# Writes of zeros on GpSimd between indirect DMAs, counted by the planner

## The chip, the cores and the metric

The kernel runs on one core of a Trainium2 chip. Five engines work side by side, each on its own queue in order: TensorE (PE) for matrix products, VectorE (DVE) and ScalarE (ACT) for elementwise work and reductions, GpSimd (POOL), and SyncE (SP), which here issues most of the DMAs. An engine waits for another through semaphores. DMAs move data between the chip's main memory and the core's SBUF, and land some time after they are issued. An *indirect* DMA takes a list of row numbers and reads or writes one row of a table per partition; in this kernel POOL issues all of those.

The metric is the time of the kernel on the device in microseconds (us), as the median of several runs. A profile is one execution that is recorded instruction by instruction; it has a time of its own.

## The reference

The input is 8 blocks of 512 tokens, each token a vector of 128 numbers. Three steps follow each other, each with a residual:

```python
x = x + 0.5 * ffn(layernorm(x))
x = x + attn(layernorm(x))
x = x + 0.5 * ffn(layernorm(x))
```

with

```python
def ffn(x):                       # 8 experts, one for each token
    xn  = rms_norm(x) * scale
    ids = argmin(distance(xn, centroids))
    for e in range(8):
        a, g = split(xn @ up_w[e])            # 128 -> 2 x 256
        y = (a * silu(g)) @ down_w[e]         # 256 -> 128
        out = where(ids == e, y, out)
    return out + x

def attn(x):                      # a decaying sum along the 512 tokens of a block
    r, k, v = split(x @ W_rkv + b_rkv)
    r, k = sigmoid(r), exp(k)
    u1, u2 = scan(lam, k * v), scan(lam, k)   # y[t] = lam * y[t-1] + u[t]
    return ((u1 + gamma * k * v) / (u2 + gamma * k + 1e-6) * r) @ W_o + b_o
```

All is in float32. A token uses one expert only, so the kernel sorts tokens by expert and computes each once.

## The kernel before, in words

**Tables.** The first ffn works on two tables of tokens (table 0 holds blocks 0 to 3, table 1 blocks 4 to 7), the second on one (table 2, all eight blocks, routed in the batches 0 and 1, 2 and 3, 4 and 5, 6, 7). For each batch the kernel normalises (moments on DVE, roots on ACT and a Newton step on POOL, L508 to L511, or DVE), compares with the centroids on PE, and ranks the tokens of each expert, which gives every token a row in a table in main memory. `scatter` (L720) writes the rows there: one indirect DMA on POOL for 128 tokens, four for each block. The tokens of an expert then lie in whole tiles of 128 rows; eight zero fills on SP (L830), at addresses that come with the last routing of a table, pad the last tile of each expert.

**Experts.** A table's tiles are worked on in pairs (`pair`). SP loads the tokens (`xg`, L892) and the expert's weights (`wup`, L899); PE transposes (L905), multiplies by the first weights (L910); ACT and DVE form `a * silu(g)` (L942, L947); PE multiplies by the second weights (L918). Pairs 0 to 11 belong to table 0, 12 to 23 to table 1, 24 to 43 to table 2, which is taken in four parts of 8, 8, 4 and 19 tiles as its batches are routed. For tables 0 and 1 the results go to a table of results through SP (L984), and `finish` gathers them back in token order: four indirect DMAs on POOL for each block (L997), then one addition on DVE (L1006). For table 2 `send` (L961) writes each tile straight to the output with one indirect DMA on POOL.

**Attention** runs between, for blocks 0 and 1, 2 and 3, 4 and 5, 6, 7: projections on PE, exponentials on ACT, two scans and eight further passes on DVE.

**The order.** No engine's order is written by hand. Each piece of work is handed to a planner (`Plan.add`) with the engines that could do it, a cost in us on each, what it reads and writes, and a lag for a DMA's landing. `Plan.schedule` simulates the five queues with these costs: it takes the piece that can start first, with a priority between those that can start nearly at once. `Plan.trace` does this for 48 settings of three parameters (how long to wait for the preferred engine, for a change of ACT's table, and how near two starts count as equal), keeps the order with the shortest simulated span, and issues the instructions in it. So a change of costs on one engine can move work on all. A scatter, a gather and a send cost 1.3 each there.

Of the kernel before, what the change touches and what calls it, by code (L numbers as in the profile page):

```python
# [10 lines left out]
F32 = mybir.dt.float32  # L11
# [8 lines left out]
class Buf:  # L20


    def __init__(self, make, tag=None):
        self.make, self.tag, self.tile = make, tag, None
        self.writers, self.readers = [], []
# [5 lines left out]


class Op:
    def __init__(self, ways, reads, writes, order, lag, table):
        self.ways, self.order, self.lag, self.table = ways, order, lag, table
        self.bufs = list(dict.fromkeys(list(reads) + list(writes)))
        self.needs, self.users = set(), []


class Plan:  # L40
# [8 lines left out]

    HOP, SWITCH = 0.1, 1.28

    def __init__(self, slots, load_table):
        self.ops, self.slots, self.load_table = [], slots, load_table

    def add(self, ways, reads=(), writes=(), order=None, part=False, lag=0.0, table=None):
        op = Op(ways, reads, writes, order or {}, lag, table)
        for b in reads:
            op.needs.update(b.writers)  # L60
            b.readers.append(op)
        for b in writes:
            op.needs.update(b.readers)
            if not (part and not b.readers):
                op.needs.update(b.writers)
            if b.readers or not part:
                b.readers, b.writers = [], []
            b.writers.append(op)
        op.needs.discard(op)
        self.ops.append(op)  # L70

    def schedule(self, spare, wait, slack):

        left, ready, uses = {}, {}, {}
        for op in self.ops:
            left[op], ready[op] = len(op.needs), 0.0
            for b in op.bufs:
                uses[b] = uses.get(b, 0) + 1
        slots = {tag: [0.0] * n for tag, n in self.slots.items()}
        free, held, released, table = {}, set(), {}, None  # L80
        waiting = [op for op in self.ops if not op.needs]
        order, span = [], 0.0
        while waiting:
            could = []
            for op in waiting:
                at = ready[op]
                for b in op.bufs:
                    if b.tag and b not in held:
                        if not slots[b.tag]:
                            break  # L90
                        at = max(at, min(slots[b.tag]))
                else:
                    for n, (engine, cost, call) in enumerate(op.ways):
                        then = max(at, free.get(engine, 0.0))
                        if n == 0 or free.get(op.ways[0][0], 0.0) > then + spare:
                            if op.table not in (None, table):
                                then += wait
                            could.append((then, engine, cost, call, op))
            if not could:
                return None  # L100
            first = min(could, key=lambda c: c[0])
            start, engine, cost, call, op = min(
                (c for c in could if c[1] == first[1] and c[0] <= first[0] + slack),
                key=lambda c: (c[4].order.get(c[1], c[4].index), c[0]),
            )
            load = None
            if op.table not in (None, table):
                load = table = op.table
                cost += max(0.0, self.SWITCH - wait)
            order.append((op, call, load))  # L110
            for b in op.bufs:
                if b.tag and b not in held:
                    slots[b.tag].remove(min(slots[b.tag]))
                    held.add(b)
            waiting.remove(op)
            free[engine] = start + cost
            end = start + cost + op.lag
            span = max(span, end)
            for b in op.bufs:
                uses[b] -= 1  # L120
                released[b] = max(released.get(b, 0.0), end)
                if uses[b] == 0 and b.tag:
                    slots[b.tag].append(released[b] + self.HOP)
            for u in op.users:
                left[u] -= 1
                ready[u] = max(ready[u], end + self.HOP)
                if left[u] == 0:
                    waiting.append(u)
        return span, order

    def trace(self):
        for i, op in enumerate(self.ops):
            op.index = i
            for n in op.needs:
                n.users.append(op)
        orders = [
            self.schedule(spare, wait, slack)
            for spare in (0.0, 0.5, 1.0, 3.0) for wait in (0.0, 0.4, 0.8, 1.28)
            for slack in (0.05, 0.1, 0.2)
        ]  # L140
        span, order = min((o for o in orders if o), key=lambda o: o[0])
        for _, call, load in order:
            if load:
                self.load_table(load)  # L144
            call()
        return span

# [2 lines left out]
def kernel(  # L150
# [37 lines left out]
    nc = tc.nc  # L188
    B, L, D = x_in.shape
    E, _, H2 = up_w.shape  # L190
    H = H2 // 2
    P = 128
# [14 lines left out]
    ROW = 2 * D + 4  # L207
# [8 lines left out]
    const = ctx.enter_context(tc.tile_pool(name="const", bufs=1))  # L216
# [79 lines left out]
    slots = {}  # L296
# [19 lines left out]

    small_d = part_of(ps_small, "d", 0, TMAX * E, 128 // (TMAX * E))
    small_r = part_of(ps_small, "r", 128, E * (TMAX + 1), RBUF)
    plan = Plan(slots, nc.scalar.preload_act_table_set)
    add = plan.add  # L320
    FIRST, LATE = -10**6, 10**6
    EXP, SILU = "natural_log_exp_and_others", "silu_and_others"
# [40 lines left out]
    rows = const.tile([E + 1, P], F32, tag="rows", name="rows")  # L363
# [177 lines left out]
    class Table:  # L541
# [33 lines left out]
        order = 0  # L575
# [74 lines left out]
    def route(table, batch, near, rows):  # L650
# [8 lines left out]
        posi = buf(route_p, [P, TMAX], I32, "posi", n, 3)  # L659
# [66 lines left out]
        for i, b in enumerate(batch):  # L726
            there = Buf(None)
            table.parts.append(there)
            row = Buf(lambda b=b: xrow[b]) if table.f else rows[i][0]
            for t in range(NT):  # L730
                add([("POOL", 1.3, lambda row=row, t=t, q=i * NT + t: scatter(row, t, q))],
                    [posi] + rows[i], [there], part=True, lag=2.4)

    def take(table, m: int):

# [137 lines left out]
    def pair(k, table, parts, keep, spots, at_, downs, downs_, tiles, start):  # L873
        n = len(tiles)
        f, row, early = table.f, table.row, table.left > 0
        xg = buf(work, [P, 2, ROW], F32, "xg", k, 7)
# [7 lines left out]
        y = buf(work, [P, 2, D], F32, "ys", k, 4)  # L884
# [38 lines left out]
        for i, j in enumerate(tiles):  # L923
            add([("SP", 0.52, lambda i=i, j=j: rows(i, j))], [at_] + parts, [xg], {"SP": LATE + k},
                part=True, lag=2.3)
        for i, j in enumerate(tiles):
            add([("SP", 0.52, lambda i=i, j=j: weights(i, j))], [at_], [wup], {"SP": LATE + k},
                part=True, lag=3.8)
# [25 lines left out]
        if f:  # L954
            add([("DVE", 0.1 + 0.18 * n, lambda: nc.vector.scalar_tensor_tensor(  # L955
                y()[:, :n, :], half(), 0.5, xg()[:, :n, D : 2 * D], ALU.mult, ALU.add))],
                [ps_y, xg], [y], soon)

            def send(i):
                nc.gpsimd.nop()  # L960
                inst = nc.gpsimd.indirect_dma_start(  # L961
                    out=out.rearrange("b l d -> (b l) d"),
                    out_offset=bass.IndirectOffsetOnAxis(
                        ap=xg()[:, i, 2 * D : 2 * D + 1].bitcast(I32), axis=0),
                    in_=y()[:, i, :], in_offset=None, bounds_check=TOKENS - 1, oob_is_err=False,
                ).ins
                tc.declare_no_dep(inst, group="out", reason="each token is in one row")
                tc.add_to_no_dep_group("out", inst)

            for i in range(n):  # L970
                add([("POOL", 1.3, lambda i=i: send(i))], [y, xg], [], lag=2.5)
            return
        add(
            [
# [17 lines left out]
    def finish(table, b: int):  # L992

        yg = buf(work, [P, NT, D], F32, "yg", b, 4)

        def gather(t):
            nc.gpsimd.indirect_dma_start(  # L997
                out=yg()[:, t, :], out_offset=None, in_=table.result()[:, :],
                in_offset=bass.IndirectOffsetOnAxis(
                    ap=table.posi[:, table.blocks.index(b), t : t + 1], axis=0),  # L1000
            )

        for t in range(NT):
            add([("POOL", 1.3, lambda t=t: gather(t))], [table.result, table.posi_], [yg], part=True,
                lag=2.0)
        add([("DVE", 0.68, lambda: nc.vector.tensor_add(xb[b], yg(), xb[b]))], [half_[b], yg], [x_[b]])  # L1006

    def attention(batch):
# [108 lines left out]
    for i, (f, batches, taken) in enumerate(TABLES):  # L1117
        Table.order = i * LATE // 8
        table = Table(f"t{i}", f, [b for batch in batches for b in batch])
# [44 lines left out]
```

## Time and profile before

| | us |
|---|---|
| median of 3 timed runs | 330.13 |
| lowest, highest | 328.52, 331.52 |
| profiled execution, its own time | 374.23 |
| its span, first to last instruction | 372.5 |
| PE busy in the span | 245.3 |
| DVE busy | 179.9 |
| ACT busy | 165.0 |
| POOL busy | 162.8 |
| of it, 135 indirect DMAs (32 + 32 + 32 + 39) | 139.7 |

The mean granted clock of PE was 0.864 of full speed in the profiled execution. Busy times are of the engine itself; SP has none, since it only issues. A line of the timeline gives start and duration in us, engine, line of the code, operation, what is written from what, shapes, and in brackets the idle time of the engine before it and what ended it. "issue" means that nothing in the profile explains the idle time; "remote" means a semaphore whose setter the profile does not show. The view of waits sums idle times by who waited and who ended it. The view by stretches gives busy times of the engines in windows of the span.

### The profile page before, as it was taken

How to read it: one execution, taken by the hardware profiler on the slowest of the kernel's cores; microseconds unless marked ns; L12 is line 12 of the kernel's file. 1: busy time of each engine (PE TensorE's matmuls, PEld its weight loads, DVE VectorE, ACT ScalarE, POOL GpSimd, SP SyncE). 2: the span in 40 equal slices, each digit the busy share in tenths (PEclk: the TensorE clock that was granted, in tenths of full speed). 3: DMA queues.
4: the chain of work that ended last, by engine and by line, in shares of the span. 5: the costliest groups of instructions: out<-in, count | busy, mean ns of one | idle time of the engine just before them, and what ended most of it. 6: DMA issues, size and time to landing. Idle time of an engine off the chain costs nothing. (4 is left out here: it accounts for less than half of the span.)

```text
span 372.5 us, 5675 instructions
## 1 busy us (share of the span) xinstructions
PE 245.3 (66%) x1510; PEld 201.6 (54%) x1510; DVE 179.9 (48%) x607; ACT 165.0 (44%) x355; POOL 162.8 (44%) x244
## 2 busy tenths in 40 slices
PE   4754635089966921998772985569971457997871
PEld 3644525089866911965351632229761356996761
DVE  4583882022211121467996979766875502232230
ACT  4881880234332301589723867634882311232230
POOL 5277457300000474110187578810277652465545
PEclk9999998569999975899987788768996577899997
DMA  8611372167767843620011125351045547787710
GB/s 225 172 43 42 89 231 76 60 195 226 209 192 234 261 138 104 189 72 28 22 37 42 35 73 171 127 143 58 0 136 186 150 168 231 242 257 230 226 56 17
DMA packets 46226, 50.25 MB, mean 135 GB/s; under 512 B 6095, under 2 KB 32739, under 8 KB 46194
## 3 DMA queue, kind: packets, MB, share of 16 engines
q1 hardware_dynamic: 41334, 39.31, 35.5%
q0 software_dynamic: 4832, 10.56, 8.4%
q8 instruction: 13, 0.21, 0.3%
q14 instruction: 19, 0.16, 0.2%
q10 hardware_dynamic: 28, 0.01, 0.0%
HBM read 36.00 MB, written 14.31 MB: 135 GB/s over the span
## 5 line engine op out<-in xcount | busy, mean ns | idle before, releaser
L910 PE MATMUL h<-xgT,wup 128*128 128x128 f32 x680 | 94.5, 295 | 11.4 <-DMA wup<-in_L_ffn_up_w_dram 7.1
L910 PEld LDWEIGHTS h<-xgT,wup 128*128 128x128 f32 x680 | 89.5, 211 | 13.9 <-issue 10.4
L947 DVE TENSOR_TENSOR sg<-h,sg 128x512 f32<-128x512 f32 (+1 forms) x44 | 29.2, 671 | 117.0 <-ACT sg L942 107.1
L997 POOL DMA_INDIRECT yg<-yt,pt x32 | 36.3, 1133 | 83.1 <-DMA xg<-t 55.7
L918 PE MATMUL ps_xy<-wsb,sg 128*128 x340 | 50.4, 294 | 32.8 <-ACT xgT L933 20.0
L918 PEld LDWEIGHTS ps_xy<-wsb,sg 128*128 128x128 f32 x340 | 44.7, 204 | 37.7 <-ACT xgT L933 25.7
L961 POOL DMA_INDIRECT out_dram<-ys,xg x39 | 38.5, 986 | 43.0 <-DVE ys L955 25.2
L942 ACT ACTIVATE sg<-h 128x512 f32<-128x512 f32 (+1 forms) x44 | 25.2, 582 | 66.8 <-PE h L910 37.9
L933 ACT ACTIVATE xgT<-ps_xy,cols 128x256 f32<-128x256 f32 (+1 forms) x44 | 20.5, 465 | 48.6 <-remote 17.3
L720 POOL DMA_INDIRECT t<-xn,posi_t x32 | 31.1, 971 | 16.2 <-issue 8.1
L720 POOL DMA_INDIRECT t<-xrow,posi_t x32 | 33.8, 1055 | 9.9 <-issue 8.2
L905 PE MATMUL ps_xy<-ident,xg 128*128 128x128 f32 x85 | 19.9, 312 | 25.0 <-ACT xgT L933 13.4
L619 PE MATMUL ps_small<-cw,xT 128*128 128x8 f32 x128 | 22.9, 309 | 10.1 <-issue 4.6
L619 PEld LDWEIGHTS ps_small<-cw,xT 128*128 128x128 f32 x128 | 21.9, 260 | 14.2 <-issue 7.5
L905 PEld LDWEIGHTS ps_xy<-ident,xg 128*128 128x128 f32 x85 | 11.9, 157 | 29.1 <-ACT xgT L933 14.1
L1105 PEld LDWEIGHTS side_o<-wo_sb,num 128*128 128x128 f32 x64 | 10.8, 243 | 16.1 <-DVE num L1070 11.6
L445 ACT ACTIVATE xrow<-x,nra,rs 128x128 f32<-128x128 f32 x32 | 13.1, 482 | 14.4 <-issue 6.7
L473 DVE BATCH_NORM_STATS2 bn_f<-x 128x6 f32<-128x128 f32 x64 | 13.5, 277 | 10.6 <-ACT x L462 6.6
L975 ACT ACTIVATE ys<-ps_xy 128x256 f32<-128x256 f32 (+1 forms) x24 | 9.0, 375 | 21.6 <-PE ps_xy L905 9.3
L1105 PE MATMUL side_o<-wo_sb,num 128*128 128x128 f32 x64 | 11.0, 328 | 10.0 <-DVE num L1070 10.0
L508 POOL TENSOR_TENSOR tr<-va,yr 128x8 f32<-128x8 f32 (+1 forms) x11 | 2.7, 241 | 30.2 <-ACT yr L500 26.1
L144 ACT ACT_TABLE_LOAD x12 | 15.4, 1283 | 0.2
(166 smaller groups left out, 382.2 us busy)
## 6 DMA issues: line engine op xcount, KB each, us to landing
wup<-in_L_ffn_up_w_dram SPq DMA_DIRECT2D x85, 256.0 KB
xg<-t SPq DMA_DIRECT2D x39, 130.0 KB
xg<-t SPq DMA_DIRECT2D x46, 64.0 KB
yt<-ys SPq DMA_DIRECT2D x22, 128.0 KB
x<-in_L_attn_inputs_dram SPq DMA_DIRECT2D x8, 256.0 KB
t<-fill SPq DMA_DIRECT2D x9, 130.0 KB
t<-fill SPq DMA_DIRECT2D x18, 64.0 KB
wsb<-in_L_ffn_down_w_dram SPq DMA_DIRECT2D x8, 128.0 KB
```

The source lines that it names most:

```text
L144: self.load_table(load)
L619: nc.tensor.matmul(ps_d()[:, ts(i * NT + t, E)], xT()[:, ts(t, P)], cw, start=True, stop=True)
L720: ordered(table, nc.gpsimd.indirect_dma_start(out=table.at()[:, :], out_offset=bass.IndirectOffsetOnAxis(ap=posi()[:, q : q + 1], axis=0), ...
L905: nc.tensor.transpose(ps_x()[:, ts(i, P)], xg()[:, i, :D], ident)
L910: nc.tensor.matmul(hp()[:, i, ts(c, P)], wup()[:, i, ts(c, P)], xgT()[:, ts(i, P)], start=True, stop=True,)
L918: nc.tensor.matmul(ps_y()[:, ts(i, D)], sg()[:, i, ts(c, P)], wdown[c][:, ds(expert(downs[j]) * W, D)], start=(c == 0), stop=(c == NHC - 1),)
L933: ("ACT", 0.2 + 0.13 * n, lambda: nc.scalar.activation(xgT()[:, : n * P], ps_x()[:, : n * P], AF.Copy, scale=scale_c)),
L942: [("ACT", 0.16 + 0.22 * n, lambda: nc.scalar.activation(sg()[:, :n, :], hp()[:, :n, H:], AF.Silu))],
L947: [("DVE", 0.1 + 0.28 * n, lambda: nc.vector.tensor_mul(sg()[:, :n, :], hp()[:, :n, :H], sg()[:, :n, :]))],
L961: inst = nc.gpsimd.indirect_dma_start(out=out.rearrange("b l d -> (b l) d"), out_offset=bass.IndirectOffsetOnAxis(ap=xg()[:, i, 2 * D : 2 ...
L997: nc.gpsimd.indirect_dma_start(out=yg()[:, t, :], out_offset=None, in_=table.result()[:, :], in_offset=bass.IndirectOffsetOnAxis(ap=table. ...
L1105: nc.tensor.matmul(ps_o()[:, ts(t, P)], num()[:, ts(i * NT + t, P)], wo_sb, start=False, stop=(t == NT - 1),)
```

## The change

The planner learns of rows of indirect DMAs. An operation has a new mark, `row`, which scatters, gathers and sends carry. While planning, a marked operation that starts less than 0.65 us after POOL came free counts as one more of a row, otherwise as the first of a new one. In front of the fifth of a row the plan puts a pause of 1.3 us on POOL and counts anew. Unmarked work on POOL in between does not by itself end a row. When the instructions are issued, a pause is a `memset` of 128 partitions by 1536 float32 zeros on POOL into a tile that nothing reads. Since the pause delays the start of the operation in the simulation, it takes part in the choice among the 48 orders, and the order on all engines is another one. In the code of the change, numbers of lines are 9 to 11 higher.

```diff
-    HOP, SWITCH = 0.1, 1.28
-
-    def __init__(self, slots, load_table):
-        self.ops, self.slots, self.load_table = [], slots, load_table
-
-    def add(self, ways, reads=(), writes=(), order=None, part=False, lag=0.0, table=None):
-        op = Op(ways, reads, writes, order or {}, lag, table)
+    HOP, SWITCH, ROW, PAUSE = 0.1, 1.28, 4, 1.3
+
+    def __init__(self, slots, load_table, pause):
+        self.ops, self.slots, self.load_table, self.pause = [], slots, load_table, pause
+
+    def add(self, ways, reads=(), writes=(), order=None, part=False, lag=0.0, table=None, row=False):
+        op = Op(ways, reads, writes, order or {}, lag, table, row)
...
-            order.append((op, call, load))
+            pause = False
+            if op.row:
+                row = row + 1 if start < free.get(engine, 0.0) + self.PAUSE / 2 else 1
+                if row > self.ROW:
+                    pause, row = True, 1
+                    start += self.PAUSE
+            order.append((call, load, pause))
...
-        for _, call, load in order:
+        for call, load, pause in order:
             if load:
                 self.load_table(load)
+            if pause:
+                self.pause()
             call()
...
-    plan = Plan(slots, nc.scalar.preload_act_table_set)
+
+    idle = const.tile([P, 3 * L], F32, tag="idle", name="idle")
+    plan = Plan(slots, nc.scalar.preload_act_table_set, lambda: nc.gpsimd.memset(idle, 0.0))
...
-                    [posi] + rows[i], [there], part=True, lag=2.4)
+                    [posi] + rows[i], [there], part=True, lag=2.4, row=True)
...
-                add([("POOL", 1.3, lambda i=i: send(i))], [y, xg], [], lag=2.5)
+                add([("POOL", 1.3, lambda i=i: send(i))], [y, xg], [], lag=2.5, row=True)
...
-                lag=2.0)
+                lag=2.0, row=True)
```

More of the change, by code (lines that the diff above doesn't have):

```diff
@@ L33, with __init__ @@
 class Op:
-    def __init__(self, ways, reads, writes, order, lag, table):
-        self.ways, self.order, self.lag, self.table = ways, order, lag, table
+    def __init__(self, ways, reads, writes, order, lag, table, row):
+        self.ways, self.order, self.lag, self.table, self.row = ways, order, lag, table, row
         self.bufs = list(dict.fromkeys(list(reads) + list(writes)))
@@ L81, in schedule @@
         waiting = [op for op in self.ops if not op.needs]
-        order, span = [], 0.0
+        order, span, row = [], 0.0, 0
         while waiting:
```

## The prediction

> **What bounds the kernel now.** I read the timed runs against the profiled execution, then the waits, then the stages one by one in the timeline. The first comparison sets the tone: the profiled execution took 374.23 us (span 372.5), the timed runs 328.52 to 331.52, median 330.13. The profiled one is 44.1 us longer, so before a wait in it is costed, it must be asked whether the timed runs have that wait at all. The view of waits, filtered to waits whose releaser the profile can't name ("remote"), with columns total, times and longest:
>
> ```profile
> ACT xgT L933 <- remote: 17.3, 1, 17.3
> ...
> ACT sg L942 <- remote: 14.2, 2, 10.1
> ...
> DVE slot_t L703 <- remote: 8.4, 2, 4.9
> ...
> ACT ys L975 <- remote: 7.9, 1, 7.9
> ...
> ACT xT L462 <- remote: 6.7, 1, 6.7
> ```
>
> They sum to 54.5 us; DVE's 4.9 and ACT's 6.7 are the same stretch (30 to 38 us), so 49.6. The timeline of ACT shows the longest, and that of POOL what runs beside it:
>
> ```profile
> 54.68 0.47 ACT L933 ACTIVATE xgT<-ps_xy,cols 128x256 f32<-128x256 f32 x1 [0.78 <-PE ps_xy L905]
> 72.47 0.47 ACT L933 ACTIVATE xgT<-ps_xy,cols 128x256 f32<-128x256 f32 x1 [17.31 <-remote]
> ```
>
> ```profile
> 44.17 1.01 POOL L720 DMA_INDIRECT t<-xn,posi_t  x1 [0.15 <-issue]
> 45.48 0.99 POOL L720 DMA_INDIRECT t<-xn,posi_t  x1 [0.30 <-issue]
> 49.65 0.96 POOL L720 DMA_INDIRECT t<-xn,posi_t  x1 [3.18 <-DVE near L642]
> 50.91 0.95 POOL L720 DMA_INDIRECT t<-xn,posi_t  x1 [0.30 <-issue]
> ```
>
> From 49.65 POOL issues 16 indirect DMAs in a row, 1.26 us apart, until 69.6. After the fourth or fifth, everything else stands: PE's transposes for the third pair are issued at 57.85, ACT answers at 72.47, when the row has ended and landed. In the same stretch register moves on SP take 0.7 us each where they take 0.03 elsewhere. The other "remote" waits also lie in or just behind POOL's rows (128 to 147 beside 16 gathers, 335 to 339 beside five sends). POOL itself keeps its 1.26 us. This is what the added writes can interrupt, and the whole forecast hangs on whether it exists without the profiler. 49.6 us of such waits and an excess of 44.1 us nearly cancel: the simplest account is that the stalls are the profiled execution's own, and that at most 5.5 us of these waits are in a timed run, if nothing else was dearer under the profile.
>
> With them taken out, the timed run is: routing to about 50; experts of the first two tables, bound by PE and the weight loads; attention, DVE 80 to 93% busy; then 16 pairs of experts as a tail.
>
> ```profile
> 80.00:90.00 10.00, 10.00 (x90) 10.00 (x90) 2.08 (x3) 4.49 (x10) 0.00 (x0) 0.99 0.72 222
> ...
> 180.00:190.00 10.00, 6.65 (x23) 2.65 (x22) 9.26 (x9) 4.94 (x8) 4.52 (x4) 0.97 0.14 40
> ...
> 350.00:360.00 10.00, 8.33 (x75) 8.14 (x74) 2.96 (x6) 2.40 (x5) 5.47 (x6) 1.00 0.43 130
> ```
>
> The columns after the length are PE, PE's weight loads, DVE, ACT and POOL. POOL bounds none of these stages through its total; it bounds the hand-overs: first expert, first attention, last send.
>
> **The change, part by part.** The price of one pause. The trace has no memset of 128x1536, but two smaller ones on POOL: 128x128 takes 0.20 us and 128x256 takes 0.30, so 0.10 per 128 columns, and 0.20 + 11 x 0.10 = 1.30 us. Their start-to-start distances (0.15 and 0.26) give 0.15 + 11 x 0.11 = 1.36. It also takes the place of the 0.30 us that POOL spends between two indirect DMAs: where four small operations stand between two of them now, 0.03 + 0.16 us are idle instead. Net 1.30 + 0.19 - 0.30 = 1.2 us. The new order holds 30 of them: 7 among the 32 scatters of the first two tables, 6 among the gathers, 9 among the last table's scatters and the sends between them, 8 in the sends behind the last scatter. That is 39 us of POOL work (its busy time from 163 to about 202), of which only what a hand-over waits for counts.
>
> *First experts.* The scatters of block 3 are re-ordered too. Now two go out early (36.45, 37.71) and two behind the Newton step that waits for ACT (43.80 to 44.02), the last ending at 46.47. In the new order all four stand behind that step, and a pause before them: 44.05 + 1.30 + 0.16 = 45.5, three more at 1.26, last end 50.2: 3.8 later. If the timed run has that Newton step earlier, POOL's row is the limit and three pauses stand in it: 3.6. SP's loads of the first pair wait for the last landing (49.39, load at 50.0), and ACT, which clears scaling work until 53.5, hides 0.5 to 1.0. I take 3; everything behind is in order on PE, so it passes through. Loads of pairs 3 and 4 also move behind the eight zero fills on SP (8 x 0.52 us); pairs 0 to 2 occupy PE for 3 x 3.4 us (1.95 + 1.06 + 0.38), which covers it.
>
> *First gathers.* Attention on blocks 0 and 1 needs eight gathers, with one pause between: 1.2, and DVE's chain starts with it. The pauses behind it (blocks 2 and 3: 2.3 to 3.5 us; second table: up to 3.5) lie beside a DVE that is 84 to 93% busy from 170 to 200. DVE waits for gathers only 7.2 us in all. I take 0, upper end 3.5.
>
> *Attention.* Here a rule of the Trainium skill and a row pull apart. Row: POOL's 128x4 multiplication at 231.87 takes 2.06 us beside DVE's scan at 231.65 (2.28 us), against 0.20 elsewhere. If a memset met the same, a pause would take up to 2.3 instead of 1.3, and the twelve near the attention would cost POOL up to 12 us more. The page "SBUF — State Buffer", section "Who interferes with whom", says that a DVE instruction with two SBUF inputs contends with a GpSimd instruction that reads SBUF, not with one that only writes it; a memset only writes. The multiplication reads, so row and rule agree on it, and no row here shows a writer. The rule names one exception, DVE copies in a two-port mode, which a running memset would block for its 1.3 us. The DVE's long work here is scans and two-input products, so I take 0, with 0 and 4 us (three meetings) as ends. Nothing in it gives time back.
>
> *Before the tail.* The new plan moves more than POOL. The up-products of pairs 24 to 27 (1.95 us each) stand later on PE, out of a stretch where PE is 95 to 100% busy (250 to 270), so the last routing may come up to 2 x 1.95 = 3.9 earlier. Against that, SP loads the eight tiles of pairs 28 to 31 behind the eight zero fills, and POOL puts the last scatter of block 5 behind six sends and three pauses. Now that scatter lands at 289.4, the loads start at 289.7 and pair 28 reaches PE at 292.7. Then, the fills wait for the last routing (written at 293.3), take 0.7 + 8 x 0.52 = 4.9, the load and landing 3.3: 301.5, or 297.6 with the 3.9 gained. The difference is 4.9 to 8.8. PE still has the moved pairs' 6 us of up-products to do in that gap, which leaves it less idle but doesn't start the tail earlier. However, in the timed run pairs 29 and 30 also wait for SP today, whose fills sit before the next weights. Ends -3 and +8; I take 2, since most of the tail's loads can't start before the last routing in either order.
>
> *Tail.* 31 sends with 8 pauses are 31 x 1.29 + 8 x 1.2 = 50 us in about 60: hidden while pairs come, except the last. The pauses stand in front of the last three sends, and the last five now run without a gap:
>
> ```profile
> 363.14 0.98 POOL L961 DMA_INDIRECT out_dram<-ys,xg  x1 [1.43 <-DVE ys L955]
> 364.43 0.98 POOL L961 DMA_INDIRECT out_dram<-ys,xg  x1 [0.30 <-issue]
> 365.71 0.98 POOL L961 DMA_INDIRECT out_dram<-ys,xg  x1 [0.30 <-issue]
> 367.00 0.98 POOL L961 DMA_INDIRECT out_dram<-ys,xg  x1 [0.30 <-issue]
> 368.29 0.98 POOL L961 DMA_INDIRECT out_dram<-ys,xg  x1 [0.31 <-issue]
> ```
>
> A pause in there moves the end by 1.2.
>
> Sum: 3 + 1.2 + 0 + 0 + 2 + 1.2 = 7.4. Against the profiled execution's own time: 374.23, less the 44.1 that the timed runs don't have, is 330.13; plus 7.4 is 337.5. I say 337. The lower ends (2.4 + 1.2 + 0 + 0 - 3 + 0) give 330.7; the upper (3.8 + 1.2 + 3.5 + 4 + 8 + 1.2 = 21.7) together 352, unlikely at once; ten to fourteen of it are 340 to 344.
>
> **The rivals.** *The stalls are real and the pauses end them* (faster). Place: the rows of more than four. Price: at most what doesn't fit into the 44.1, 5.5 us of the named waits, and beside them SP's fills from 298.25 to 306.5, which take 8.3 instead of 4.2 and hold back pairs 29 to 31, say 4 more; 337 less about 10 is 327, and with the reorder falling well 324. For it: behind the short row of 44.17 to 46.47 nothing stalls. Against: a Newton step of 1.1 us between two rows (29.7 to 30.8) did not end the stall of 31 to 37.7, 0.7 us per register move looks like recording, and the timed runs are shorter by nearly the whole sum. It decides once real stalls exceed 11 us. 12%; I place it at 325.
>
> *The pauses fall where POOL waits anyway* (no difference): seven of the tail's eight do, and the plan has counted them, so it may have moved the rest there. What is left is 1.2 + 1.2 or less: 331 to 333, taken as 332. Against: the block 3 scatters. 21%.
>
> *The re-ordered tail is the main cost*: pair 28 late by the full 8 us on top of 5.4: 343.5 to 345. 17%.
>
> *The likeliest*, 334 to 341, named 337: 50%. That the change doesn't do what it says is small: the 30 writes stand in POOL's order.
>
> Within 1% is 326.8 to 333.4, about what a measurement of this kernel can tell from no change. From the cases: faster 0.11, same 0.22, slower 0.67. The range 328 to 345 leaves out most of the faster rival and the worst reorder.
>
> **What would show it.** In the changed profile: 30 memsets of about 1.3 us; fewer or shorter "remote" waits, and so a profiled time that falls, perhaps under 360, while the timed median rises; the first expert transposes some 3 us later relative to the last Newton step of the first table; eight zero fills ahead of the loads of pair 28; a gap of 1.5 us before the last three sends. A fall of the timed median together with the profiled one would prove me wrong on whose the stalls are; a rise over 345 would mean that memsets and DVE collide, or that the tail waits for SP's fills longer than I allow.

## The result, and the profile after

The changed kernel takes 347.92 us (median of four runs, 343.79 to 348.0). The kernel before takes 329.32 beside it (four runs, 328.29 to 331.52). The ratio is 1.0525, with a 95% interval of 1.0427 to 1.0622: about 18.6 us slower. The forecast was 337, with a range of 328 to 345. The direction was right, the size was too small by more than half.

The page of the changed kernel, by busy time and by groups of instructions (group: line, engine, operation, operands, count; then busy us and mean ns; then the idle time before):

```profile
span 346.3 us, 5698 instructions
...
PE 242.7 (70%) x1510; PEld 200.0 (58%) x1510; DVE 185.3 (54%) x607; ACT 165.7 (48%) x355; POOL 202.5 (58%) x274
...
L330 POOL MEMSET idle<- 128x1536 f32 x30 | 42.0, 1401 | 0.0
```

There are 30 memsets of 1.40 us, 42.0 us together, and POOL's busy time is up by 39.7. The profiled execution took 348.0 us, as long as the timed ones: where the profiled execution of before was 44 us longer than its timed runs, this one is not. No wait with releaser "remote" is left. ACT's copy of the third pair, which waited 17.31 us, now follows without a wait (start, duration, what):

```profile
63.98 0.47 ACT L944 ACTIVATE xgT<-ps_xy,cols 128x256 f32<-128x256 f32 x1
```

If only the two profiles are compared, the change makes the kernel 26 us faster. The timed runs say the opposite. PE's mean granted clock was 0.882 and PE was busy for 242.7 us; a second profile of the kernel before (e5, below) has 0.890 and 243.5, so a slower PE is not what makes the kernel longer. The stages, in the same columns as in the prediction (PE, its weight loads, DVE, ACT, POOL, then PE's granted clock, DMA share, GB/s); first a stretch of the attention before, then the same stage after, then two of the tail after:

```profile
200.00:210.00 10.00, 4.71 (x13) 3.02 (x14) 7.77 (x29) 6.13 (x16) 7.89 (x11) 0.50 0.16 46
...
180.00:190.00 10.00, 4.49 (x15) 3.07 (x16) 6.51 (x27) 5.91 (x16) 8.49 (x11) 0.54 0.14 39
320.00:330.00 10.00, 8.46 (x73) 8.02 (x73) 2.47 (x6) 3.21 (x6) 8.15 (x9) 1.00 0.79 230
330.00:340.00 10.00, 5.57 (x46) 5.04 (x44) 3.11 (x7) 1.35 (x3) 8.45 (x9) 0.97 0.11 34
```

In this part of the attention POOL was as busy as DVE before (7.89 and 7.77) and is ahead of it now (8.49 and 6.51). In the other stretches from 150 to 240 DVE still is the busier one, except from 210 to 220 (8.10, POOL 8.98). In the tail POOL is at 8.15 and 8.45 of 10 us; as each indirect DMA of 0.98 us is followed by 0.30 us in which POOL waits for nothing, that is a full queue. The end of POOL's timeline:

```profile
336.94 0.98 POOL L972 DMA_INDIRECT out_dram<-ys,xg  x1 [0.30 <-issue]
337.91 1.42 POOL L330 MEMSET idle<- 128x1536 f32 x1
339.49 0.99 POOL L972 DMA_INDIRECT out_dram<-ys,xg  x1 [0.17 <-issue]
...
342.07 0.98 POOL L972 DMA_INDIRECT out_dram<-ys,xg  x1 [0.30 <-issue]
```

From one send to the next it is 1.29 us, with a memset between 2.55: a pause costs 1.26 net, where the prediction had 1.2. PE began its last products at 335.4. The sends are a backlog by then.

### The profile page after: what moved, and what is told of

Its sections match the earlier page's. It is cut to its first block, busy times and chain, and to the rows that moved or that the text cites. A ratio compares the mean times of both kernels' runs of the same rounds, so it can differ in the third digit from the quotient of the medians.

```text
span 346.3 us, 5698 instructions
## 1 busy us (share of the span) xinstructions
PE 242.7 (70%) x1510; PEld 200.0 (58%) x1510; DVE 185.3 (54%) x607; ACT 165.7 (48%) x355; POOL 202.5 (58%) x274
## 4 chain that ended last, share of the span: by engine, by line
PE 27%; DMA 17%; DVE 15%; POOL 14%; ACT 11%; issue 9%; SPq 4%; POOLq 1%; ACTq 0%; DVEq 0%
PE h L921 11%; DMA wup<-in_L_ffn_up_w_dram 5%; DMA xg<-t 5%; POOL t L731 5%; PE ps_xy L929 4%; PE ps_small L630 4%; ACT xrow L456 4%; DMA out_dram<-ys,xg 3%; POOL out_dram L972 3%; POOL idle L330 2%; PE ps_xy L916 2%; POOL yg L1008 2%; SPq L903 2%; ACT L151 2%; DMA yg<-yt,pt 1%
## 5 line engine op out<-in xcount | busy, mean ns | idle before, releaser
L921 PE MATMUL h<-xgT,wup 128*128 128x128 f32 x680 | 89.8, 288 | 8.0 <-DMA wup<-in_L_ffn_up_w_dram 8.0
L921 PEld LDWEIGHTS h<-xgT,wup 128*128 128x128 f32 x680 | 85.8, 204 | 10.5 <-issue 6.7
L1008 POOL DMA_INDIRECT yg<-yt,pt x32 | 34.0, 1061 | 65.3 <-DMA wup<-in_L_ffn_up_w_dram 41.9
L929 PEld LDWEIGHTS ps_xy<-wsb,sg 128*128 128x128 f32 x340 | 45.5, 207 | 20.5 <-issue 14.8
L330 POOL MEMSET idle<- 128x1536 f32 x30 | 42.0, 1401 | 0.0
L630 PE MATMUL ps_small<-cw,xT 128*128 128x8 f32 x128 | 24.3, 321 | 10.0 <-ACT xT L473 7.5
L630 PEld LDWEIGHTS ps_small<-cw,xT 128*128 128x128 f32 x128 | 23.4, 277 | 12.1 <-ACT xT L473 9.0
L1116 PEld LDWEIGHTS side_o<-wo_sb,num 128*128 128x128 f32 x64 | 11.3, 255 | 18.1 <-DVE num L1081 14.0
L1116 PE MATMUL side_o<-wo_sb,num 128*128 128x128 f32 x64 | 11.7, 342 | 11.5 <-DVE num L1081 11.5
L456 ACT ACTIVATE xn<-x,nra,rs 128x128 f32<-128x128 f32 x32 | 13.1, 481 | 8.5 <-DVE nra L612 5.6
```

Source lines behind the costliest of these rows:

```text
L330: plan = Plan(slots, nc.scalar.preload_act_table_set, lambda: nc.gpsimd.memset(idle, 0.0))
L456: nc.scalar.activation(out()[:, t, :], src()[:, t, :], AF.Identity, bias=bias()[:, t : t + 1], scale=scale()[:, t : t + 1],)
L630: nc.tensor.matmul(ps_d()[:, ts(i * NT + t, E)], xT()[:, ts(t, P)], cw, start=True, stop=True)
L921: nc.tensor.matmul(hp()[:, i, ts(c, P)], wup()[:, i, ts(c, P)], xgT()[:, ts(i, P)], start=True, stop=True,)
L929: nc.tensor.matmul(ps_y()[:, ts(i, D)], sg()[:, i, ts(c, P)], wdown[c][:, ds(expert(downs[j]) * W, D)], start=(c == 0), stop=(c == NHC - 1),)
L1008: nc.gpsimd.indirect_dma_start(out=yg()[:, t, :], out_offset=None, in_=table.result()[:, :], in_offset=bass.IndirectOffsetOnAxis(ap=table. ...
```

## The experiments

Three groups: order against pauses, which pauses, and what else the findings allow. All runs compute the whole reference, and the memsets write a tile that nothing reads. The kernel before had a median of 327.95, 326.94 and 328.42 in the three groups.

### Order or pauses

**e1_order_only**: the new order, no memset issued.

```diff
         for call, load, pause in order:
             if load:
                 self.load_table(load)
-            if pause:
-                self.pause()
             call()
```

> The changed kernel's order on every engine, but no memset is issued: all 30 pauses are counted by the planner and none is executed. Theory A (the new order is the main cost: the loads of pair 28 behind eight zero fills, the last scatter of block 5 behind six sends, the PE gap of some 14 us ahead of the tail): 339 to 345. Theory B (the pauses themselves are the main cost: they stand in POOL's way at the hand-overs and make POOL the bound of the tail): 329 to 334. On the stalls: if they are the profiled execution's own and come from long rows of indirect DMAs, this kernel has its rows back, so its profiled execution is some 30 to 45 us longer than its timed runs.

Measured: 331.57 us, ratio 1.0107 (1.006 to 1.0155), so 3.6 us (2.0 to 5.1) for the new order. Theory B holds, and the rival of the re-ordered tail falls. The expectation on the stalls fell too: the profiled execution took 331.34, as the timed ones, though its rows are long again.

**e2_pauses_only**: the order before on every engine, the memsets issued.

```diff
                 if row > self.ROW:
                     pause, row = True, 1
-                    start += self.PAUSE
```

> The order of the kernel before on every engine, with a memset of 128x1536 ahead of the fifth indirect DMA of each row (24 of them), which the planner doesn't count. Theory A (order): 331 to 337, since only a pause that a hand-over waits for costs. Theory B (pauses): 342 to 348. If the stalls seen in the profile before were real in the timed runs as well, this kernel has the rows broken without the new order and should be faster than before, 315 to 327. If they are the profiled execution's own, its profiled time falls to within 3 us of its timed one.

Measured: 346.62, ratio 1.0589 (1.0524 to 1.0655): 18.7 us for 24 memsets that together take 33.5 us. The cost is more than half of POOL's added work, and 13 of the 24 memsets stand in the chain of work that ended last in its profile. Breaking the rows gains nothing on balance, so the timed runs show no sign of the stalls.

**e3_pauses_sends** and **e4_pauses_rest**: as e2, but only sends, or only scatters and gathers, carry the mark.

```diff
-                add([("POOL", 1.3, lambda i=i: send(i))], [y, xg], [], lag=2.5, row=True)
+                add([("POOL", 1.3, lambda i=i: send(i))], [y, xg], [], lag=2.5)
```

(e4; e3 takes the mark from `scatter` and `gather` instead.)

> The order before, with memsets of 128x1536 only in rows of sends (4 of them, all in the tail). Theory B in the form that POOL bounds the tail: 334 to 338 (4 x 1.3 us on a queue that already has no slack, plus what it started with). Theory A, or POOL hidden in the tail as the prediction had it: 330 to 332, one pause's 1.2 us at the end at most.

> The order before, with memsets of 128x1536 only in rows of scatters and gathers (20 of them). The prediction's terms for the first experts (3) and the first gathers (1.2) make 334. If later gathers and the routings behind them count too: 336 to 342. If the tail alone is what pauses cost: 330 to 332.

Measured: 330.62 for the four among sends (1.0098, 1.007 to 1.0127) and 344.61 for the 20 others (1.049, 1.0433 to 1.0547). By the ratios that is 3.2 us for the sends and 16.1 for the rest. e4 is above all three of its expectations: most of the cost lies before the tail, and in more than what the prediction had priced there. e3's time lies where a tail that hides most of its pauses was to lie, but against its own before it is 3.2 us for pauses that add 5.0 (4 x 1.26), more than the one pause at the end that the prediction let through; two of the four stand in its profile's chain. Nor are four pauses the changed kernel's eight, which e9 tries.

### The profile of before, once more

**e5_before_again**: the kernel before, unchanged, for a second profile.

> The kernel before, unchanged. If long rows of indirect DMAs stall the other engines under the profiler (the prediction's reading), its profiled execution is again some 40 us longer than the timed runs, 365 or more. If the 374 was an accident of that one execution, it is 325 to 332. The kernel with the changed order and no pause, and the one with pauses among the sends alone, have long rows and did not stall, so the second is expected.

Measured: 329.06, span 327.3. The 374 was an accident of one execution. None of the thirteen other profiles of this case, long rows or not, has a "remote" wait. What caused it in that one is open: it was seen once. It also hid what the other views show. Here is the chain of work that ended last, by engine, first as the stalled profile had it, then of e5:

```profile
issue 5%; PE 3%; DMA 2%; SPq 2%; POOL 2%; ACT 1%; another core or an unknown queue 1%; DVE 1%; POOLq 0%; ACTq 0%; DVEq 0%
```

```profile
PE 30%; DMA 23%; POOL 14%; ACT 10%; DVE 9%; issue 8%; SPq 4%; ACTq 0%; POOLq 0%; DVEq 0%
PE h L910 11%; DMA xg<-t 7%; POOL yg L997 6%; PE ps_xy L918 5%; DMA wup<-in_L_ffn_up_w_dram 5%; POOL t L720 4%; DMA t<-xrow,posi_t 3%; PE ps_small L619 3%; DMA out_dram<-ys,xg 3%; SPq L892 2%; DMA t<-xn,posi_t 2%; PE side_o L1105 2%; PE ps_xy L905 2%; ACT xrow L445 2%; PE side_o L1101 2%
```

The shares of the first line add up to 17% of the span: the chain broke off at an unknown releaser near the end, so it said nothing of the stages before. In e5 it is whole, and POOL holds 14% of the span, 46 us, with gathers (`yg`) and scatters (`t`) in the middle of the kernel. A pause ahead of any of these can move the end. This view of e5, between 201 and 221 us, is the clearest (start, us, what):

```profile
201.21 2.11 POOL t L720
203.33 1.11 POOL tr_a L508
204.51 2.07 POOL tr_a L509
206.65 1.12 POOL tr_a L510
207.84 1.11 POOL rn L511
209.10 1.00 POOL t L720
210.41 1.05 POOL t L720
211.76 0.96 POOL t L720
213.02 1.71 POOL t L720
215.04 3.04 DMA t<-xrow,posi_t
218.87 2.21 DMA xg<-t
221.12 0.48 PE ps_xy L905
```

The scatters of table 2's first batches, with a Newton step between them, run on a full POOL until 216.5; their last landing starts the load of pair 24, and that its transposes. This is a hand-over like the three that the prediction named, and it isn't among them.

### Which pauses

**e6_pauses_first_scatters**, **e7_pauses_gathers**, **e8_pauses_last_scatters**: e4 in three parts. Scatters of tables 0 and 1 have kind 1, those of table 2 kind 2, gathers kind 3; the counting is that of e4, and only one kind is issued (6, 6 and 8 memsets).

```diff
                 if row > self.ROW:
-                    pause, row = True, 1
-                    start += self.PAUSE
+                    pause, row = op.row == 2, 1
...
-                    [posi] + rows[i], [there], part=True, lag=2.4, row=True)
+                    [posi] + rows[i], [there], part=True, lag=2.4, row=2 if table.f else 1)
```

> The order before; memsets only among the scatters of tables 0 and 1 (6). The prediction's term for the first experts, passed on: +3, so 331. If the experts behind it take the delay up (in the kernel with pauses among all scatters and gathers a lag of 2.75 us at the first transposes has fallen to 0 at the end of table 0): 327 to 329.

> The order before; memsets only among the gathers (6). The prediction's terms (first gathers 1.2, later gathers 0): 329. If POOL is on the path through both tables' gathers, each of the six counts about in full, 6 x 1.25 = 7.5, so 334 to 337.

> The order before; memsets only among the scatters of table 2 (8). The prediction had no term for these but for the last hand-over before the tail: 328 to 330. If POOL is on the path through these scatters as well, six or seven of the eight count: 335 to 338. The three kernels with a part each add up to about the 16.7 us of the kernel with all 20 if nothing hides.

| pauses among | number | median | ratio | 95% | us |
|---|---|---|---|---|---|
| first tables' scatters (e6) | 6 | 329.98 | 1.0063 | 1.0028 to 1.0099 | 2.1 |
| gathers (e7) | 6 | 331.97 | 1.0118 | 1.0048 to 1.0188 | 3.9 |
| table 2's scatters (e8) | 8 | 336.23 | 1.0272 | 1.0185 to 1.0359 | 8.9 |
| sends (e3) | 4 | 330.62 | 1.0098 | 1.007 to 1.0127 | 3.2 |

(us: the ratio less one, by the before of the group.) e6 and e7 fell between their two expectations; in e8 the second held. The parts add up to 18.1 us; e2, with all of them, has 19.3 by the same reckoning, so within the intervals they simply add. Table 2's scatters are nearly half: 8.9 us, where eight pauses of 1.26 us are 10.1. Not all of it need pass through POOL's queue, as the last part shows. In e8's chain between 197 and 217 the memset lies in the row itself:

```profile
208.71 1.00 POOL t L730
209.71 1.39 POOL idle L329
211.26 0.97 POOL t L730
```

### The tail, and the length of a pause

**e9_after_no_tail**: the changed kernel without its last eight pauses, those behind the last scatter.

```diff
+        left = sum(pause for _, _, pause in order) - 8
         for call, load, pause in order:
             if load:
                 self.load_table(load)
-            if pause:
+            if pause and left > 0:
                 self.pause()
+            left -= pause
```

> The changed kernel in its own order, without the last eight of its 30 pauses, those among the sends behind the last scatter. If the tail hides them but for the last, as the prediction had it: 1.2 us less than the changed kernel, so 346 to 347. If POOL has become the bound of the tail (its sends follow each other without waiting from about 306 on, and it ends some 5 us behind PE): 3 to 4 us less, 343.5 to 345.

Measured: 343.25 (343.21 to 348.11), ratio 1.0491 (1.0387 to 1.0595). That is 4.7 us below the changed kernel by the medians and just under its second expectation, but four runs each can't settle it: the intervals overlap, one of e9's runs took 348.11 and one of the changed kernel's 343.79, and in the profiles 2.2 us of the difference arise before the tail. Their timelines tell the tail apart. In e9 the last products begin at 333.17 and the last send at 336.89:

```profile
336.89 0.98 POOL L974 DMA_INDIRECT out_dram<-ys,xg  x1 [0.30 <-issue]
```

That is 3.7 us, as in e1 (321.56 and 325.28), and 6.7 in the changed kernel (335.38 and 342.07). By these profiles the eight pauses cost 3.0 at the end, not 1.2.

**e10_pauses_tiny**: as e2, with a memset of 128x4.

```diff
-    plan = Plan(slots, nc.scalar.preload_act_table_set, lambda: nc.gpsimd.memset(idle, 0.0))
+    plan = Plan(slots, nc.scalar.preload_act_table_set, lambda: nc.gpsimd.memset(idle[:, 0:4], 0.0))
```

> The order before, with 24 memsets at the same places as in the kernel with pauses only, but of 128x4 zeros (about 0.1 us). If the time is the length of the pauses on POOL: within 1.5 us of before, 326 to 329. If an operation of another kind between indirect DMAs costs something by itself (the descriptors of a row being prepared ahead, say), a good part of the 18.7 us stays: 332 or more.

```profile
L329 POOL MEMSET idle<- x24: 99/120/149, 24.8 to 317.8; 128x4 f32 x24
```

Measured: 328.67, ratio 0.9998 (0.9969 to 1.0028). (The line: shortest, median, longest in ns; first and last start.) Here another operation in a row is free; its length is what costs. At 0.12 us it fits into the 0.30 us that stand between two indirect DMAs anyway.

### What the finding is good for

**e11_newton_dve** and **e12_pool_costs**: if POOL's queue is on the path, the Newton steps in it are too.

```diff
-        add([("POOL", 1.2, lambda: newton(nc.gpsimd)), ("DVE", 0.8, lambda: newton(nc.vector))],
+        add([("DVE", 0.8, lambda: newton(nc.vector))],
             [va, y], [rs, t], {"POOL": FIRST, "DVE": FIRST})
```

(e12 keeps both ways, with 2.4 instead of 1.2 for POOL, and 1.5 instead of 1.3 for a gather.)

> The kernel before, with the Newton steps of the roots allowed on DVE alone, so that POOL does nothing but indirect DMAs after its start; the planner makes a new order of it. If POOL's queue is on the path between gathers and scatters (there a Newton step of four small operations takes 5.4 us beside DVE's scans), 2 to 5 us less than before: 322 to 325. If DVE bounds those stages, its added 0.8 us for each of some 12 steps and the new order make it 329 to 335.

> The kernel before, with POOL's costs in the planner nearer to the trace: a Newton step on POOL 2.4 instead of 1.2, a gather 1.5 instead of 1.3. Nothing else is changed, but the order is a new one. If the planner, told of POOL's true costs, relieves it at the hand-overs: 322 to 326. If orders differ by chance more than by this: 327 to 334, as the changed order without pauses did with 331.6.

Measured: 319.3 for e11 (0.9727, 0.9658 to 0.9795) and 321.71 for e12 (0.981, 0.9735 to 0.9884). Both are faster than both kernels, e11 by 9.1 us against before, more than was expected, and e12 by 6.7. In e11's page POOL's part of the chain has gone from 14% to 2%:

```profile
span 317.2 us, 5719 instructions
...
PE 35%; DVE 19%; DMA 17%; ACT 13%; issue 7%; SPq 6%; POOL 2%; POOLq 0%; DVEq 0%
```

The step that took POOL from 203.33 to 208.95 in e5 takes DVE 0.73 us right behind a scan in e11:

```profile
194.04 2.28 DVE L1075 TENSOR_TENSOR_SCAN den<-lam_l,kT 128x1024 f32<-128x1024 f32 x1
196.24 0.14 DVE L508 TENSOR_TENSOR tr_a<-van,yr_a 128x4 f32<-128x4 f32 x1
...
196.81 0.16 DVE L511 TENSOR_TENSOR rn<-tr_a,yr_a 128x4 f32<-128x4 f32 x1
```

How much of the 9.1 us is this, and how much a luckier order, was not separated, in e12 neither. In e11 POOL also issues 32 indirect DMAs from 153.60 to 199.66 without another operation, and nothing stalls.

## Why the prediction was wrong, step by step

The ladder shows where the changed kernel falls behind e1, which has the same order without memsets (starts in us in the two profiles, and the lag). The last column is the lag of e9, which is the changed kernel up to the tail, and shows how far two executions differ.

| | e1 | after | lag | e9 |
|---|---|---|---|---|
| first expert's transpose | 54.78 | 58.49 | 3.7 | 3.6 |
| first gather | 109.49 | 114.76 | 5.3 | 3.3 |
| first scan of the attention | 145.68 | 151.70 | 6.0 | 3.3 |
| first scatter of table 2 | 186.67 | 194.27 | 7.6 | 5.8 |
| 16th scatter of table 2 | 215.19 | 227.47 | 12.3 | 9.8 |
| last scatter | 275.82 | 289.30 | 13.5 | 10.7 |
| last send | 325.28 | 342.07 | 16.8 | 11.6 |

With the order's own 2.2 between the profiles (e5 327.3, e1 329.5) the 16.8 make the whole difference of 346.3 to 327.3. A single profile is not exact: e5's own time, 329.06, is 1 to 2 us above the medians of the timed runs of before.

The pauses reach the end in two ways. One is POOL's queue: seven pieces of memsets, 8.6 us, stand in the chain that ended last in the changed kernel. The other was tried by none of the experiments, but the traces show it: a memset also holds DVE. Ahead of the first experts the changed kernel reads as in the first three lines, and e1, with the same order, as in the last two:

```profile
46.84 2.00 DVE L718 CAST posi_t<-best_t 128x8 int32<-128x8 f32 x1
46.92 1.92 DVE L653 TENSOR_TENSOR near<-ps_small,rs 128x64 f32<-128x64 f32 x1
47.41 1.40 POOL L330 MEMSET idle<- 128x1536 f32 x1
...
44.98 0.17 DVE L716 CAST posi_t<-best_t 128x8 int32<-128x8 f32 x1
45.06 0.21 DVE L651 TENSOR_TENSOR near<-ps_small,rs 128x64 f32<-128x64 f32 x1
```

The cast ends with the memset (48.84 and 48.81), and what stands behind it in DVE's queue ends with it too. It had begun 0.57 us ahead of the memset, and why it was held from then on is not shown. Eight of the 30 memsets have such a group of longer DVE instructions beside them; the first of each group is a cast or a `TENSOR_SCALAR` (one tensor with scalars). Nothing of the kind is in e10, whose memsets take 0.12 us. Five of these holds stand in the changed kernel's chain:

```profile
32.30 0.98 DVE posi_t L718
41.46 1.01 DVE one L616
46.92 1.92 DVE near L653
177.53 1.05 DVE va L603
267.70 1.65 DVE posi_t L718
```

In e1 the same five take 0.16 to 0.21 each, so 5.7 us more: with the 8.6 of the memsets, 14.3 of the 16.8. No run separates the two ways, since both go with the length of a memset. What a chain names are releasers inferred from semaphores, so the shares are estimates.

- **The stalls are the profiled execution's own**: right where it mattered. The timed runs never had them, and breaking the rows gained nothing (e2); the rival that ended on the faster side falls. But the link to rows of more than four is wrong (e1, e5, e11), so the changed profile without stalls is no effect of the change.
- **One pause, net 1.2**: right for POOL's queue; 1.40 each, 1.26 net. What a pause does to DVE was not in the price.
- **First experts, 3**: near in size, by luck. The prediction had the scatters' row as the limit. The pauses make 3.6 to 3.7 at the first transposes, but the first loads are issued only 0.95 us later than in e1 (49.98 and 49.03); the chain leads over DVE, and the first three holds above make 3.4. The order adds 4.7 there (50.11 in e5, 54.78 in e1), which the prediction had not seen, and the experts behind give part of it back: at the first gather the changed kernel is 6.7 behind e5, e9 4.8.
- **First gathers 1.2, later gathers 0 (upper 3.5)**: the first cost 0 to 0.8 up to the scan. From there to the first scatter of table 2 the lag grows by 1.6 to 2.6, of which 0.9 is the first pause of table 2's own scatters (1.48 us between the Newton step and the scatter, 0.55 in e1); 0.7 to 1.6 is left for the later gathers. In the old order gathers cost 3.9 together (e7). The 0 was too low: the argument was DVE's 84 to 93% and its 7.2 us of waiting for gathers in the stalled profile; in e5 it waits 11.7.
- **Attention, 0**: the rule held for what POOL pays. Beside DVE's scans and two-input products POOL's multiplication takes 2.06 us again while the memsets on either side of it, which only write, keep 1.40, as the Trainium skill says of a writer ("SBUF — State Buffer", section "Who interferes with whom"):

```profile
207.44 2.29 DVE L1086 TENSOR_TENSOR_SCAN den<-lam_l,kT 128x1024 f32<-128x1024 f32 x1
208.08 1.40 POOL L330 MEMSET idle<- 128x1536 f32 x1
...
211.69 2.06 POOL L520 TENSOR_TENSOR tr_a<-tr_a,yr_a 128x4 f32<-128x4 f32 x1
...
220.26 1.40 POOL L330 MEMSET idle<- 128x1536 f32 x1
```

  The 0 left out what DVE pays. The exception that the prediction names, a memset that blocks a DVE copy, it weighed against the attention's scans and products alone. It came true for casts and `TENSOR_SCALAR` operations, once in the chain while the attention ran (177.53, 0.9 us) and four times in the routing outside it, where it had no term at all. Which mode these operations ran in, no trace shows.
- **The step that failed**: "POOL bounds none of these stages through its total; it bounds the hand-overs: first expert, first attention, last send." From this the nine pauses among table 2's scatters and the sends between got no price of their own. With the 0.9 above they cost 4.9 to 5.6 up to the 16th scatter, and some 1 more up to the last, which includes the hold at 267.70; alone, in the old order, 8.9 (e8). It is the largest term of all. There is a hand-over for every batch that is routed: its scatters must have landed before its experts can start, and the next attention's Newton step queues between them.
- **Before the tail, 2**: the sequence was as described, and pair 28 begins 4.5 us later in e1 than in e5 (268.09 and 263.64). In the changed kernel's chain the fills go first, then the load of pair 28:

```profile
273.09 0.54 SPq L841
274.33 3.15 DMA t<-fill
278.40 2.22 DMA xg<-t
280.67 0.49 PE ps_xy L916
```

  The new order as a whole costs 3.6 us in the timed runs; in the profiles e1 is 0.2 behind e5 at the 16th scatter of table 2 and 2.2 at the last send. So the 2 was about right, and of the two rivals that were given 21% and 17%, no difference and the re-ordered tail as the main cost, neither is the case.
- **Tail, 1.2**: 3.0. The work of 50 us was right (31 x 1.29 + 8 x 1.26). The room was not: "about 60" came from the stalled profile (59.8). In e5 the sends behind the last scatter run from 276.21 to 324.02, 47.8 us, and in e1 they take as long. The pauses overflow it by 2.3.

So the missing term for table 2's scatters is 6 to 7 us, the tail was 2 too low and the later gathers about 1: some 9 of the 11.2 us by which the forecast fell short; the rest is not assigned. What memsets did to DVE is contained in these and in the first experts.

The tail's error comes from reading slack in an execution that was 44 us too long: the prediction took the 44 us off the total, but not out of the stage. The largest error does not come from there. The stalled profile is 28.3 us behind e5 at the first scan, 30.4 at the last scatter and 45.3 at the last send, so all but 2 us of the stalls lie outside the attention and the routing of table 2. From the first to the 16th scatter of table 2 it took 28.87 us, e5 28.97. From 190 to 240 it has POOL busy for 6.05 to 8.98 of each 10 us, and the scatters with the Newton step between them stood in its timeline. The prediction showed the one stretch from 180 to 190, with 4.52, and the chain, which is followed back from the end, broke off before it came to these hand-overs.

## What to carry to other kernels

A profile whose own time is far from the timed runs is to be replaced before it is read: the total can be mended by a subtraction, the slack in a stalled stage can't, and a chain of waits whose shares add up to 17% has nothing to say on the other 83. An engine at 50% of the span may be full for whole stages; where each batch's result passes through its queue, most of the time put into it counted (8.9 of 10.1 us in e8), elsewhere less (2.1 of 7.6 in e6). Work put on one engine as a filler can hold another, so its price has to be looked for there too. And a planner's order depends on its costs: with a step entered at 1.2 us that takes 5.4 beside a scan, it made an order that two others beat by 2 to 3%, one with truer costs and one without that step on POOL. That truer costs make better orders in general is not shown by two.

## What was not expected of the hardware

- One execution of a kernel can stall its engines for some 44 us in all (register moves on SP 0.7 us each where they take 0.03), while none of the thirteen other profiles, the same kernel's second one among them, shows it.
- A `memset` on POOL can hold casts and `TENSOR_SCALAR` operations on DVE until it ends. In eight places of the changed kernel 0.17 us became up to 2.00 (the cast at 46.84), and what followed in DVE's queue was held as well. A scan that was under way when the memset came was not longer for it (2.29 us at 207.44 and at 211.47, the second beside no memset).
- POOL leaves 0.30 us between two indirect DMAs even with nothing to wait for, and a memset of 0.12 us put there cost nothing (0.9998, 0.9969 to 1.0028).
- Not only POOL's arithmetic but its indirect DMAs are longer beside DVE's scans. Over the fourteen profiles, the 85 that share more than 0.3 us with a scan of over 1 us take 1.7 us on average and up to 3.03; the 1664 that share no more than that with any DVE instruction of over 1 us take 0.98. An example is the one of 2.96 in e11 (at 158.25, beside a scan of 2.27). Why was not isolated.
